# Two attention layers on one core: order of the two products that fill a tile of scores

## The chip, the cores and the metric

The kernel runs on one core of a Trainium2 chip. The metric is the device time of one execution in microseconds (us), lower is better. Three executions of the kernel before took 4043.36, 4045.41 and 4047.82 us; the median, 4045.41 us, is what the change is measured against.

## The reference, cut to what matters

Two residual layers are applied to an array of 4 images of 32 by 32 positions with 768 channels in float32. Each layer normalises in groups, makes q, k and v for 12 heads of 64 channels (the second layer also convolves and normalises each of them), and attends over the 1024 positions of an image, with a bias that depends on the row and the column of query and key:

```python
attn = jnp.einsum('bqd,bkd->bqk', q, k) / np.sqrt(HD)
rel_bias_h = jnp.einsum('bhwc,hkc->bhwk', rq, Rh)
rel_bias_w = jnp.einsum('bhwc,wkc->bhwk', rq, Rw)
attn = (attn.reshape(b * NH, h, w, h, w) + rel_bias_h[:, :, :, :, None] + rel_bias_w[:, :, :, None, :]).reshape(b * NH, hw, hw)
attn = jax.nn.softmax(attn, axis=-1)
out = jnp.einsum('bqk,bkd->bqd', attn, v)
```

The score before the softmax is thus a sum of two terms, q by k and a bias. The change concerns the order in which the kernel adds these two.

## The kernel before, in words

The work is cut into 48 pairs of heads (4 images, 2 layers, 6 pairs of 2 heads; 128 partitions hold the 64 channels of both heads). For each pair, `attend` (L614) runs over two halves of 512 queries (index `c`), and in each half over 8 tiles of 128 keys (index `kt`), in two groups of four tiles. So there are 96 halves, 192 groups and 768 tiles.

One tile of scores, `s`, lies in PSUM (pool `ps_s`, two buffers, L75 and L667): 128 keys by 2 heads by 512 queries. TensorE fills it with two products for each head. The first (L669) is q by k: plain float32, 64 channels deep, one head in the upper and one in the lower half of the array's rows. It starts the accumulation. The second (L671) adds the biases: the stationary operand `ones` holds zeros and ones that pick, for a key, its row and its column of the bias table, and the moving operand `bias` holds the tables. Both are of type float32r, and the bias was split (L528) into a high part and a rest, so that one product is exact enough. It closes the accumulation, and its end lets ScalarE take the exponential of the whole tile (`e`, L676). As `s` has two buffers, the third tile of a group waits until the exponential of the first has read its buffer, and the fourth until that of the second has.

The biases come late in a pair's preparation. `positions` (L502) makes them on TensorE from q, ScalarE copies them to `whole` (L522), `split` makes `high` (ScalarE, L533) and the rest (VectorE, L534), and 8 DMAs on GpSimd's queue for each half of the queries (L544) spread them over the partitions of `bias` (two buffers, L538). The first tile of a half needs four of these DMAs, the third two more, the fifth the last two.

The order of the work is written out by hand (`manual_schedule`, L94): TensorE executes the instructions in program order. Each step of `attend` yields, and after each yield pieces of other work (the next pair's projections, `positions`, `split`, the previous image's output projection) are put in from a table of events. So a group of four tiles stands between such pieces. `attend` then goes on to add up `e` on VectorE (L684) and to multiply it by v on TensorE (L690). These products and the projections use the array in two halves of columns and all 128 rows, the tiles of scores two halves of rows and all 128 columns.

Of the kernel before, what the change touches and what calls it, by code (L numbers as in the profile page):

```python
# [45 lines left out]
def two_layers(ctx: ExitStack, tc: tile.TileContext, keep, x_in, wqkv, wproj, rels, windows, vrow, small, const, onehot, picks, out):  # L46
# [19 lines left out]
    nc = tc.nc  # L66
# [12 lines left out]
    def bank(name):  # L79
        return ps_m.tile([P, 512], F32, tag="bank", name=name)  # L80
# [20 lines left out]
    def col(c, lo=0, hi=P):  # L101
        return sm[lo:hi, c : c + 1]
# [511 lines left out]
    def attend(pair, os):  # L614


        q, k, bias = pair.q, pair.k, pair.bias
        os.append(q)
        nonlocal found
        heads = [slice(j * D, (j + 1) * D) for j in range(2)]  # L620

        def more():
            nonlocal found
            if rest:
                found = rest.pop(0)(*found)

        for c in range(T // QC):
            cols = slice(c * QC, (c + 1) * QC)

            def copy(av):  # L630
                weighed = one.tile([P, QC], F32, tag="weighed", name="weighed")
                nc.scalar.copy(weighed, av)  # L632
                return weighed

            def sums(weighed, acc, c=c):

                z = bank("z")
                for j in range(2):
                    nc.tensor.matmul(  # L639
                        z[j * D : (j + 1) * D, :], cst[:, ONES : ONES + D], acc[:, j, :],  # L640
                        start=True, stop=True,
                    )
                at = 2 * (pair.i * (T // QC) + c)
                t = work.tile([P, QC], F32, tag="t", name="t", bufs=1)
                inv = work.tile([P, QC], F32, tag="inv", name="inv", bufs=1)
                nc.scalar.activation(t, z, AF.Copy, accum_out=seen[:, at : at + 1])

                nc.scalar.activation(inv, t, AF.Ln, bias=tiny)
                nc.scalar.activation(inv, inv, AF.Exp, scale=-1.0, accum_out=seen[:, at + 1 : at + 2])
                return weighed, t, inv  # L650

            def result(weighed, t, inv, cols=cols):

                nc.vector.scalar_tensor_tensor(t, t, -1.0, inv, ALU.mult, ALU.mult)
                nc.vector.scalar_tensor_tensor(inv, t, 2.0, inv, ALU.add, ALU.mult)

                if pair.layer:
                    nc.vector.tensor_tensor(inv, weighed, inv, ALU.mult)
                    nc.vector.scalar_tensor_tensor(q[:, cols], inv, col(LN + 4), q[:, cols], ALU.mult, ALU.add)
                else:  # L660
                    nc.vector.tensor_tensor(q[:, cols], weighed, inv, ALU.mult)

            for g in range(0, NKT, 4):
                es = []
                for kt in range(g, g + 4):
                    keys = slice(kt * P, (kt + 1) * P)
                    ps = ps_s.tile([P, 2, QC], F32, tag="s", name="s")  # L667
                    for j, rows in enumerate(heads):
                        nc.tensor.matmul(ps[:, j, :], k[rows, keys], q[rows, cols], start=True, stop=False)  # L669
                    for j, rows in enumerate(heads):  # L670
                        nc.tensor.matmul(  # L671
                            ps[:, j, :], ones[rows, keys], bias[c][rows, kt // 2, :],
                            start=False, stop=True,
                        )
                    e = work.tile([P, 2, QC], F32, tag="e", name="e", bufs=4)
                    nc.scalar.activation(e, ps, AF.Exp)  # L676
                    es.append(e)
                more()
                if g == 0:
                    av = ps_av.tile([P, QC], F32, tag="av", name="av")  # L680
                    acc = work.tile([P, 2, QC], F32, tag="acc", name="acc", bufs=1)
                    nc.vector.tensor_tensor(acc, es[0], es[1], ALU.add)  # L682
                for e in es[2 * (g == 0) :]:
                    nc.vector.tensor_tensor(acc, acc, e, ALU.add)  # L684
                yield
                yield
                for t, e in enumerate(es):
                    kt = g + t
                    for j in range(2):
                        nc.tensor.matmul(  # L690
                            av[j * D : (j + 1) * D, :], pair.vt[:, kt, j * D : (j + 1) * D], e[:, j, :],
                            start=(kt == 0), stop=(kt == NKT - 1),
                        )
                more()
                if g + 4 == NKT:
                    rest.extend((sums, result))
                    found = (copy(av), acc)
                yield
                yield
# [70 lines left out]
    for i, pair in enumerate(pairs):  # L770
        for _ in attend(pair, oss[i // NC]):
            for piece in events.pop(step, ()):
                piece()
            step += 1
# [309 lines left out]
```

## Time and profile before

| what | value |
|---|---|
| median of three runs | 4045.41 us |
| the profiled execution's own time | 4040.44 us |
| span of the profiled execution | 4038.7 us |
| granted TensorE clock, mean | 0.996 |
| TensorE busy with matmuls | 3945.2 us (98%) |
| VectorE, ScalarE, GpSimd busy | 2494.3, 1812.1, 409.8 us (62%, 45%, 10%) |
| q by k, L669 | 3072 records, 831.8 us |
| biases, L671 | 1536 records, 615.6 us |
| exponentials, L676 | 768 of 1023 ns, 781.3 us |

The span lies inside the time of the same execution; 1.7 us lie around it. PE is TensorE's matmul stream, PEld its loads of the stationary operand, which run beside it. A plain float32 product leaves two matmul records, each with a load of its own, a float32r product leaves one: hence 3072 records of q by k and 1536 of the biases for 768 tiles and two heads. A record's length holds waiting inside the array too; distances between starts are the safer reading.

### The profile page before, as it was taken

What the parts mean: (1) busy time and instruction counts of PE and PEld (TensorE: products, weight loads), DVE (VectorE), ACT (ScalarE), POOL (GpSimd) and SP (SyncE); (2) the same over time, 40 slices, a digit from 0 to 9 for tenths busy, and PEclk for the clock granted to TensorE, in tenths of its full rate; (3) what the DMA queues carried; (4) which work ended last, traced back from release to release, by engine and by line L of the source; (5) the groups of instructions that cost most, each with busy time, mean ns of one, the idle gap of its engine ahead of it and who ended that gap; (6) DMA issues with size and microseconds to landing.
All of it is one profiled execution on the core that took longest, in us unless ns stands there. A gap on an engine that the chain in (4) does not pass through costs nothing.

```text
span 4038.7 us, 79929 instructions
## 1 busy us (share of the span) xinstructions
PE 3945.2 (98%) x35098; PEld 1720.3 (43%) x35098; DVE 2494.3 (62%) x2800; ACT 1812.1 (45%) x2669; POOL 409.8 (10%) x776
## 2 busy tenths in 40 slices
PE   7999999999999999999899999999999999999999
PEld 3534444434344444444444344354343444434443
DVE  2455423558489985799633454245575898848883
ACT  2444424545255553455423544244443555525552
POOL 0111100110000110010011110001100011000010
PEclk9999999999999999999999999999999999999999
DMA  5333242221411222212133222422114112131112
GB/s 160 85 112 113 71 128 73 57 65 38 132 48 38 76 52 75 63 49 69 41 103 88 58 70 63 144 58 70 47 53 127 37 43 53 40 104 43 38 47 75
DMA packets 179046, 293.34 MB, mean 73 GB/s; under 512 B 22528, under 2 KB 77952, under 8 KB 178688
## 3 DMA queue, kind: packets, MB, share of 16 engines
q1 hardware_dynamic: 117248, 187.41, 14.8%
q0 software_dynamic: 61440, 100.71, 10.9%
q8 instruction: 279, 4.57, 0.5%
q14 instruction: 79, 0.65, 0.1%
HBM read 153.36 MB, written 34.01 MB: 46 GB/s over the span
## 4 chain that ended last, share of the span: by engine, by line
PE 85%; DVE 8%; ACT 3%; issue 1%; DMA 1%; POOL 0%; DVEq 0%; SPq 0%; ACTq 0%
PE qkv L85 18%; PE av L690 14%; PE s L669 14%; PE proj L85 12%; PE m3m L85 4%; PE m4m L85 4%; PE m1m L85 4%; PE s L671 3%; PE ln_c L85 3%; PE rel L517 3%; PE z L639 2%; DVE shared L459 2%; DVE acc L684 2%; PE m L85 2%; ACT e L676 2%
## 5 line engine op out<-in xcount | busy, mean ns | idle before, releaser
L676 ACT ACTIVATE e<-s 128x1024 f32<-128x1024 f32 x768 | 781.3, 1023 | 529.8 <-PE s L671 503.7
L669 PE MATMUL s<-q,k 64*128 64x512 f32 x3072 | 831.8, 618 | 27.9 <-ACT e L676 22.2
L684 DVE TENSOR_TENSOR acc<-acc,e 128x1024 f32<-128x1024 f32 x576 | 705.4, 1225 | 184.4 <-ACT e L676 133.4
L85 PE MATMUL qkv<-xn,wqkv_t 128*64 128x512 f32 x3648 | 815.6, 596 | 2.8 <-DVE xn L268 2.6
L459 DVE SCALAR_TENSOR_TENSOR shared<-shared,sm 128x1056 f32<-128x1056 f32 x576 | 758.3, 1316 | 14.9
L671 PE MATMUL s<-bias,ones 64*128 64x512 f32 x1536 | 615.6, 794 | 13.9 <-DMA bias<-whole 9.5
L690 PE MATMUL av<-e,vt 128*64 128x512 f32 x2624 | 594.5, 595 | 0.0
L544 POOL DMA_DIRECT2D bias<-high x384 | 204.1, 552 | 3356.5 <-ACT high L533 3097.9
L85 PE MATMUL proj<-q,wproj_t 128*64 128x512 f32 x2304 | 504.9, 593 | 0.0
L85 PEld LDWEIGHTS qkv<-xn,wqkv_t 128*64 128x64 f32 x3648 | 252.9, 137 | 488.5 <-issue 482.6
L669 PEld LDWEIGHTS s<-q,k 64*128 64x128 f32 x3072 | 255.4, 186 | 362.0 <-ACT e L676 210.6
L442 ACT ACTIVATE shared<-qkv,sm 128x512 f32<-128x512 f32 (+1 forms) x288 | 129.2, 501 | 595.6 <-PE qkv L85 595.6
L723 DVE SCALAR_TENSOR_TENSOR x<-proj,pbias,x 128x512 f32<-128x512 f32 x96 | 72.1, 751 | 439.4 <-PE proj L85 435.0
L690 PEld LDWEIGHTS av<-e,vt 128*64 128x64 f32 x2624 | 184.7, 137 | 347.5 <-issue 328.9
L682 DVE TENSOR_TENSOR acc<-e 128x1024 f32<-128x1024 f32 x96 | 117.6, 1225 | 345.4 <-ACT e L676 344.6
L85 PEld LDWEIGHTS proj<-q,wproj_t 128*64 128x64 f32 x2304 | 163.7, 137 | 313.5 <-issue 311.7
L671 PEld LDWEIGHTS s<-bias,ones 64*128 64x128 f32 x1536 | 150.2, 188 | 199.6 <-issue 193.6
L544 POOL DMA_DIRECT2D bias<-whole x384 | 204.9, 562 | 119.5 <-DVE whole L534 109.0
L632 ACT COPY weighed<-av 128x512 f32<-128x512 f32 x96 | 56.3, 586 | 329.2 <-PE av L690 329.2
L85 PEld LDWEIGHTS ln_c<-cst,shared 128*64 128x64 f32 x2304 | 131.4, 138 | 44.4 <-issue 34.6
L517 PEld LDWEIGHTS rel<-q,rel 64*32 64x32 f32 x6144 | 111.6, 105 | 78.0 <-issue 61.0
L85 PE MATMUL ln_c<-cst,shared 128*64 128x128 f32 x2304 | 139.2, 274 | 3.1 <-DVE shared L459 3.1
(119 smaller groups left out, 3613.0 us busy)
## 6 DMA issues: line engine op xcount, KB each, us to landing
bias<-high POOLq DMA_DIRECT2D x384, 128.0 KB, 2.8
bias<-whole POOLq DMA_DIRECT2D x384, 128.0 KB, 3.0
wqkv_t<-in_wqkv SPq DMA_DIRECT2D x78, 384.0 KB, 3.1
wqkv_t<-mixed SPq DMA_DIRECT2D x66, 384.0 KB, 3.1
wproj_t<-in_wproj SPq DMA_DIRECT2D x48, 384.0 KB, 3.7
wqkv_t<-in_wqkv SPq DMA_DIRECT2D x66, 192.0 KB, 2.5
xn<-in_x SPq DMA_DIRECT2D x24, 512.0 KB, 7.8
x<-in_x SPq DMA_DIRECT2D x48, 256.0 KB, 2.8
```

Of the source, the lines that this page charges most:

```text
L85: nc.tensor.matmul(ps[lo : lo + D], a[:, lo : lo + D], b, start=start, stop=stop, **kw)
L442: nc.scalar.activation(self.pad[s][:, rows, there : there + src.shape[2]], src, AF.Identity, bias=col(self.column(s)))
L459: nc.vector.scalar_tensor_tensor(y, window, tap, y, ALU.mult, ALU.add)
L517: nc.tensor.matmul(ps[lo : lo + S, k * S : (k + 1) * S].rearrange("p (b c) -> p b c", b=2), rel[rows, 2 * self.layer + i, first : first + ...
L544: nc.gpsimd.dma_start(sets, some.unsqueeze(1).to_broadcast([D // 2, 2, QC]))
L639: nc.tensor.matmul(z[j * D : (j + 1) * D, :], cst[:, ONES : ONES + D], acc[:, j, :], start=True, stop=True,)
L669: nc.tensor.matmul(ps[:, j, :], k[rows, keys], q[rows, cols], start=True, stop=False)
L671: nc.tensor.matmul(ps[:, j, :], ones[rows, keys], bias[c][rows, kt // 2, :], start=False, stop=True,)
L676: nc.scalar.activation(e, ps, AF.Exp)
L682: nc.vector.tensor_tensor(acc, es[0], es[1], ALU.add)
L684: nc.vector.tensor_tensor(acc, acc, e, ALU.add)
L690: nc.tensor.matmul(av[j * D : (j + 1) * D, :], pair.vt[:, kt, j * D : (j + 1) * D], e[:, j, :], start=(kt == 0), stop=(kt == NKT - 1),)
```

## The change

The biases' product of both heads is put ahead of q by k in each tile. It now opens the accumulation, and q by k closes it. Nothing is added or removed; the four matmuls of a tile, their operands and all that stands around the tile stay as they were.

```diff
@@ -666,12 +666,12 @@
                     keys = slice(kt * P, (kt + 1) * P)
                     ps = ps_s.tile([P, 2, QC], F32, tag="s", name="s")
                     for j, rows in enumerate(heads):
-                        nc.tensor.matmul(ps[:, j, :], k[rows, keys], q[rows, cols], start=True, stop=False)
-                    for j, rows in enumerate(heads):
                         nc.tensor.matmul(
                             ps[:, j, :], ones[rows, keys], bias[c][rows, kt // 2, :],
-                            start=False, stop=True,
+                            start=True, stop=False,
                         )
+                    for j, rows in enumerate(heads):
+                        nc.tensor.matmul(ps[:, j, :], k[rows, keys], q[rows, cols], start=False, stop=True)
                     e = work.tile([P, 2, QC], F32, tag="e", name="e", bufs=4)
                     nc.scalar.activation(e, ps, AF.Exp)
```

After the change the biases' product stands on L669 to L672 and q by k on L674. Compiled, the order of instructions on VectorE, ScalarE, GpSimd and SyncE is the same as before; on TensorE the matmuls of each tile change places. The waits move with the places: the wait for a free buffer of `s` and the waits for the biases' DMAs now stand together on the first biases' product of a tile.

## Prediction

> **What bounds the kernel now.** I read the page first (busy time, chain, groups), then the timeline of an ordinary group of tiles, then the waits on the biases' line, then the timeline of a tile whose biases came late.
>
> ```profile
> PE 3945.2 (98%) x35098; PEld 1720.3 (43%) x35098; DVE 2494.3 (62%) x2800; ACT 1812.1 (45%) x2669; POOL 409.8 (10%) x776
> ...
> PE 85%; DVE 8%; ACT 3%; issue 1%; DMA 1%; POOL 0%; DVEq 0%; SPq 0%; ACTq 0%
> ...
> L676 ACT ACTIVATE e<-s 128x1024 f32<-128x1024 f32 x768 | 781.3, 1023 | 529.8 <-PE s L671 503.7
> L669 PE MATMUL s<-q,k 64*128 64x512 f32 x3072 | 831.8, 618 | 27.9 <-ACT e L676 22.2
> ```
>
> TensorE is busy for 98% of the span and carries 85% of the chain that ended last; ScalarE has room. So what lengthens TensorE's stream lengthens the kernel, and what only makes ScalarE start later costs where TensorE waits for it. An ordinary group (start, length):
>
> ```profile
> 2606.86 0.60 PE L85 MATMUL proj<-q,wproj_t 128*64 128x512 f32 x2
> 2607.38 0.30 PEld L669 LDWEIGHTS s<-q,k 64*128 64x128 f32 x4 [0.81 <-issue]
> ...
> 2607.92 0.19 PEld L671 LDWEIGHTS s<-bias,ones 64*128 64x128 f32 x2 [0.24 <-issue]
> ...
> 2608.35 0.42 PEld L669 LDWEIGHTS s<-q,k 64*128 64x128 f32 x4 [0.23 <-issue]
> 2608.58 1.02 PE L669 MATMUL s<-q,k 64*128 64x512 f32 x4
> 2608.78 2.12 ACT L676 ACTIVATE e<-s 128x1024 f32<-128x1024 f32 x2 [5.85 <-PE s L671]
> ...
> 2609.86 0.30 PEld L669 LDWEIGHTS s<-q,k 64*128 64x128 f32 x4 [0.66 <-ACT e L676]
> ...
> 2612.24 0.19 PEld L639 LDWEIGHTS z<-acc,cst 128*64 128x64 f32 x3 [0.56 <-issue]
> ```
>
> Here are four intervals. From the group's first load to the first exponential: 2608.78 - 2607.38 = 1.40 us. The exponential (1.02) and 0.05 of release later, at 2609.86, the third tile begins: it waits for ScalarE, so a later first exponential makes a later third tile. From there to the first load of other work: 2612.24 - 2609.86 = 2.38. And at the top, the end of float32 work: from the last start (2606.86) to a load in another arrangement of the array 0.52; the reader of that product (VectorE, in the same window) starts at 2607.50, 0.64 after. Over all 192 groups the two tile intervals have medians of 1.40 and 2.38; in 72 groups the first is longer, since ScalarE is still on other work. Which late biases there are, from the answer for L671:
>
> ```profile
>   DMA bias<-high: 10.2, 5
>   DMA bias<-whole: 9.5, 4
> ```
>
> 19.7 us over nine waits, always the first tile of a pair. One of them:
>
> ```profile
> 407.91 1.13 PE L669 MATMUL s<-q,k 64*128 64x512 f32 x4
> ...
> 411.08 0.21 PEld L671 LDWEIGHTS s<-bias,ones 64*128 64x128 f32 x2 [2.87 <-issue]
> 411.11 0.50 PE L671 MATMUL s<-bias,ones 64*128 64x512 f32 x2 [2.07 <-DMA bias<-whole]
> 411.19 0.45 PEld L669 LDWEIGHTS s<-q,k 64*128 64x128 f32 x4
> 411.41 1.02 PE L669 MATMUL s<-q,k 64*128 64x512 f32 x3
> ...
> 411.64 2.11 ACT L676 ACTIVATE e<-s 128x1024 f32<-128x1024 f32 x2 [3.03 <-PE s L671]
> ...
> 411.88 0.59 PE L669 MATMUL s<-q,k 64*128 64x512 f32 x1
> ```
>
> q by k ran at 407.91, inside the wait for the DMA; after the landing only the biases' pass was left: 411.64 - 411.08 = 0.56 to the exponential. This is also the one place where the trace shows a biases' product with nothing ahead of it, as each group will begin after the change: from its load to the last q by k start of the product behind it 411.88 - 411.08 = 0.80.
>
> **What the Trainium skill says.** "FP8 and Floating Point Precision", TensorE Precision Notes: true float32 takes four passes, the reduced form reads a truncated value. The trace agrees: two float32 records lie 0.43 apart (two passes each), the biases' pass takes 0.23 at most (2608.35 to 2608.58). "TensorE: Matmul & The Clock Gate", Step-by-step: loads are pulled ahead of running matmuls, matmuls keep program order. The trace agrees: q's load at 2608.35 runs under the biases' pass; and keeping order means that a biases' product which waits holds up q by k behind it. "TensorEngine Tiling (Array Packing)", Key Properties: a change of the tiling mode drains the array. The trace agrees: 0.52 from a last float32 start to the next mode's load, where its passes take 0.43. "TensorE: Matmul & The Clock Gate", What's actually happening: after an idle window of about 3.4 us the clock halves until a busy one. The trace's clock record has stretches of 3.41 us at 0.5, among them just after the waits at 57 and 3930 us.
>
> **The change part by part.**
>
> *Passes.* A tile keeps two float32 records and one pass per head; in an unbroken run tiles follow every 1.09 us (exponentials at 1.09), in either order. Cost nothing; what differs is the two ends and the waits.
>
> *Group start to first exponential.* Before 1.40. After: a biases' load with nothing ahead, 0.80 to the last q by k start, then 0.64 to the reader: 1.44. The 0.80 holds 0.03 by which the second head trailed the first there (it trails by 0.01 elsewhere). Whether it trails so where there was no DMA wait, no row shows: 1.41 to 1.44. Raising every group's interval to these values, those where ScalarE is late anyway left as they are, gives 1.3 to 4.9 us over 192 groups.
>
> *Third tile to the next work.* Before 2.38. After: 0.80 + 1.09 (the fourth tile) + 0.52 = 2.41, without the trailing 2.38. Times 192: 0 to 6.3 us. The weight load of the fourth tile's biases is released by the second exponential, as q's was; it is late by at most 0.01, up to 1.5 us. With the line above: 1.3 to 12.7 us. I take 8, the trailing in the tiles that stand behind a wait and not in all others.
>
> *Late biases.* I laid the landing of the DMAs beside the first load of every tile that needs them. In ten pairs the last of the four landed after the tile's start. In six (3.0 to 5.4 us late, one 1.0) q by k filled the wait; now it comes after: load to exponential 0.57 becomes 1.44, 0.87 each, 5.2 us. In four, 0.5 us late, the biases' load stood 0.59 after the start and was wholly hidden under q by k (exponential still at 1.40). Now 0.59 + 1.44 - 1.40 = 0.63 each, 2.5 us. Sum 7.8 us (7.7 before rounding each). Queued behind the waiting instruction on TensorE are q by k, the other tiles, and all later pieces; ScalarE's exponential and VectorE's sums wait for it. The next-closest landing is 4.0 us ahead of its tile: no other pair is touched. All third and fifth tiles have at least 2 us.
>
> *The clock.* With q by k gone from the wait TensorE idles about 1 us longer in the six. Two of these already end at half clock (a 3.41 us window at half speed costs at most 1.7 us); three others idle 2.0, 2.0 and 2.9 us now and 3.0 to 3.9 then. Bounds 0 to 5.1 us; I take one new window, 1.7.
>
> *What may be gained.* Four first tiles wait 2.2 us in all for k (ScalarE, L419); a biases' pass may run under such a wait, at most 4 x 0.23 = 0.9 us, but two of the four are late-bias pairs where it can't. I count nothing. The biases' buffer comes free a product earlier for GpSimd's DMAs; they feed the second half of the queries, which has slack. Other DMAs and queues are not moved past anything.
>
> *Waits of the sequencer.* The extra event waits for the DMAs (four per half, 0.05 us each in the trace) stood behind q by k and were hidden. They now stand at the tile's head; TensorE's sequencer was seen about 0.5 us ahead of the array, so I count nothing. If the cover is gone: 384 x 0.05 = 19.6 us.
>
> *Sum.* 8 + 7.8 + 1.7 = 17.5 us. On the profiled execution, 4040.4 (span 4038.7 and 1.7 around it), that is 4057.9; that execution lies 5.0 under the median of the runs shown, so against the median 4045.4 + 17.5 = 4062.9, said as 4063.
>
> **The rivals.** A measurement of this kernel can tell about 0.2%, 8.1 us, from no change.
>
> *Not slower: the order is neutral and the lost cover is given back.* Place: the ten late tiles. If TensorE after such a tile soon has to wait for ScalarE or VectorE anyway (93 us of the span are idle), the 7.8 us vanish into that wait; with no trailing the group part is 1.3, and up to 0.9 is gained at k. It decides once less than half of the late-tile cost survives and no trailing shows. For it: 72 groups are held by ScalarE. Against: in nine of the ten the third tile began 1.08 after the first exponential began, released by it, so the delay is passed on. Time 4045.4 + 1.3 = 4047; chance 0.20, most within 0.2%, 0.03 faster.
>
> *More: event waits exposed.* At a group's head behind tiny matmuls (40 groups follow `positions`) the sequencer may have no lead. With half of the 19.6 us and all three clock windows: 8 + 7.8 + 5.1 + 9.8 = 30.7, 4076. Chance 0.12. Against: the trace shows the lead.
>
> *The change is not done.* The compiled order on TensorE shows the products swapped in all tiles; I give it nothing.
>
> **How the numbers follow.** Forecast 4063 with 0.68 (its bounds 9.1 to 25.6 us: 4054 to 4071), not slower 4047 with 0.20, more 4076 with 0.12. Slower by over 0.2%: 0.68 + 0.12 = 0.80; within: 0.17; faster: 0.03. Range 4048 to 4075: it leaves out about 0.12 of the rival below and 0.07 above.
>
> **What would show it.** In the profile after: the exponential's releaser is q by k; group start to exponential 1.41 to 1.44, third tile to next work 2.38 to 2.41 (trailing or not); a late tile's biases' load to exponential 1.44 where it was 0.57; waits on the biases' DMAs in ten first tiles totalling about 27 us where nine made 19.7 (six grow by 0.96, the load and two passes that ran inside them, and the four of 0.5 show); one to three more half-clock stretches. I am wrong if the group intervals shrink, if landings move with the order, or if event waits show at tile heads.

## The result, and the profile after

The changed kernel takes 4052.34 us (median of 15 runs, 4048.41 to 4055.28), the kernel before, timed beside it, 4043.36 us (15 runs, 4040.16 to 4047.82). The ratio is 1.0022, with a 95% interval of 1.0014 to 1.0029: 9.0 us slower, between 5.7 and 11.7. The forecast was 17.5 us slower. The profiled execution took 4052.07 us with a span of 4050.2 us, 11.5 us over the span of before.

The page after, the lines that answer to those of before:

```profile
PE 3946.5 (97%) x35098; PEld 1717.0 (42%) x35098; DVE 2494.8 (62%) x2800; ACT 1811.2 (45%) x2669; POOL 410.0 (10%) x776
...
PE 84%; DVE 9%; ACT 3%; DMA 2%; issue 2%; POOL 0%; DVEq 0%; SPq 0%; ACTq 0%
```

TensorE's busy time grew by 1.3 us, the span by 11.5: the difference is mostly idling, and DMA has gone from 1 to 2% of the chain that ended last. An ordinary group, the one that was shown of before (start, length), in which ScalarE's exponentials are now released by q by k (L674):

```profile
2616.42 0.60 PE L85 MATMUL proj<-q,wproj_t 128*64 128x512 f32 x2
2616.95 0.19 PEld L669 LDWEIGHTS s<-bias,ones 64*128 64x128 f32 x2 [0.81 <-issue]
...
2617.29 1.02 PE L674 MATMUL s<-q,k 64*128 64x512 f32 x4
...
2618.36 2.11 ACT L676 ACTIVATE e<-s 128x1024 f32<-128x1024 f32 x2 [5.86 <-PE s L674]
...
2619.43 0.19 PEld L669 LDWEIGHTS s<-bias,ones 64*128 64x128 f32 x2 [0.87 <-ACT e L676]
...
2621.80 0.20 PEld L639 LDWEIGHTS z<-acc,cst 128*64 128x64 f32 x4 [0.76 <-issue]
```

First load to first exponential: 2618.36 - 2616.95 = 1.41 us (before 1.40). Third tile to the next work: 2621.80 - 2619.43 = 2.37 (before 2.38). From the group's first load to the next work it is 4.85 us here and 4.86 before; over all groups but those behind a late wait the median is 4.86 in both kernels. The order of the two products is free here. The waits on the biases' line:

```profile
  DMA bias<-whole: 18.2, 9
  DMA bias<-high: 11.4, 3
```

This is 29.6 us in the view where it was 19.7. Neither sum is the time lost: pair 0 stands twice in each, with its weight load and with its matmul, and three of the nine waits of before (one of the twelve after) are waits of about 0.2 us in other tiles. Counted once, on the matmuls of the first tiles, five tiles waited 13.9 us before and ten wait 23.7 us after.

A pair is called late where the last of the four DMAs that its first tile needs lands after that tile's start in the trace of before. There are ten; in six of them (pairs 0, 5, 23, 24, 29 and 47) the wait is deep, 1.0 us or more, and in four it is 0.5 us. The late tile that was shown of before (pair 5):

```profile
409.28 0.21 PEld L669 LDWEIGHTS s<-bias,ones 64*128 64x128 f32 x2 [3.95 <-issue]
409.31 0.50 PE L669 MATMUL s<-bias,ones 64*128 64x512 f32 x2 [3.10 <-DMA bias<-whole]
...
409.62 1.87 PE L674 MATMUL s<-q,k 64*128 64x512 f32 x4
...
411.52 1.02 ACT L676 ACTIVATE e<-s 128x1024 f32<-128x1024 f32 x1 [4.67 <-PE s L674]
```

From the biases' load to the exponential 411.52 - 409.28 = 2.24 us, where before it was 0.56. The four q by k that follow the load take 1.87 us, where the same four take 1.02 in the ordinary group. The cause is the clock. The view of stretches of the same execution shows it (length; busy time of PE, PEld, DVE, ACT and POOL; granted clock; DMA share; GB/s):

```profile
409.70:413.10 3.40, 3.40 (x14) 1.71 (x10) 3.30 (x3) 1.02 (x1) 2.11 (x5) 0.50 0.96 245
```

The granted clock is 0.50 right after the wait. The clock record of a trace holds such stretches at 0.50, each of 3.41 us or a small multiple of it, but for the one at the trace's end; they are called half-clock stretches below, and their sums are taken over the profiled execution.

I followed the start of each group's last exponential from one trace to the other. The kernel after falls behind at all ten late pairs: these ten steps add up to 14.2 us. Between them the distance mostly stands still; from pair 9 to pair 22 it changes by less than 0.1 us over 54 groups. Against the 14.2 stand some -3 us net at seven other groups, two of which lose 1.2 and 1.3 us and the others gain. Half-clock stretches lie there in one execution and not in the other (the one at 325 us in the trace of before has no counterpart after), and waits for VectorE change. At 325.65 us of before, a product of the preparations had waited 2.93 us for VectorE (L330); after, at 326.31, it waited 2.02. So 0.9 of the 1.6 us that had been lost until then vanished in a wait that was there anyway.

### The profile page after: what moved, and what is told of

Its sections match the earlier page's. It is cut to its first block, busy times and chain, and to the rows that moved or that the text cites. A ratio compares the mean times of both kernels' runs of the same rounds, so it can differ in the third digit from the quotient of the medians.

```text
span 4050.2 us, 79929 instructions
## 1 busy us (share of the span) xinstructions
PE 3946.5 (97%) x35098; PEld 1717.0 (42%) x35098; DVE 2494.8 (62%) x2800; ACT 1811.2 (45%) x2669; POOL 410.0 (10%) x776
## 4 chain that ended last, share of the span: by engine, by line
PE 84%; DVE 9%; ACT 3%; DMA 2%; issue 2%; POOL 0%; DVEq 0%; SPq 0%; ACTq 0%
PE qkv L85 18%; PE av L690 13%; PE s L674 12%; PE proj L85 12%; PE s L669 5%; PE m4m L85 4%; PE m3m L85 4%; PE m1m L85 4%; PE ln_c L85 3%; PE rel L517 2%; DVE shared L459 2%; DVE acc L684 2%; PE z L639 2%; PE m L85 2%; ACT e L676 2%
## 5 line engine op out<-in xcount | busy, mean ns | idle before, releaser
L674 PE MATMUL s<-q,k 64*128 64x512 f32 x3072 | 793.8, 594 | 1.1 <-issue 1.1
L669 PE MATMUL s<-bias,ones 64*128 64x512 f32 x1536 | 456.4, 589 | 51.7 <-ACT e L676 21.0
L669 PEld LDWEIGHTS s<-bias,ones 64*128 64x128 f32 x1536 | 147.0, 186 | 454.1 <-ACT e L676 285.6
L674 PEld LDWEIGHTS s<-q,k 64*128 64x128 f32 x3072 | 297.3, 188 | 84.4 <-issue 49.8
```

The costliest lines, as they stand in the source:

```text
L669: nc.tensor.matmul(ps[:, j, :], ones[rows, keys], bias[c][rows, kt // 2, :], start=True, stop=False,)
```

## The experiments

Theory 1, formed on the two traces: the whole cost sits in the ten first tiles whose biases come late; the q by k that filled the wait now follows it, and the longer idling brings stretches of half clock. The rivals: a cost in every group, as the prediction's largest term had it, masked by something else; or the clock alone. Each run was timed beside the kernel before, on the same chip, and its ratio is the one to that kernel.

**1 and 2. The old order in the first tile of a pair alone, and the new order there alone.** Both kernels have the two products as functions and choose for each tile:

```diff
+                    a, b = (biases, scores) if c or kt else (scores, biases)
+                    a(True, False)
+                    b(False, True)
```

> The changed kernel, with the old order (q by k first) in the first tile of each of the 48 pairs alone; 720 of 768 tiles keep the biases first. Theory 1 (the whole cost sits in the ten first tiles whose biases come late, about 0.87 us in six and 0.63 in four, plus the clock after longer idling): 4043.4, as the kernel before, within 2 us either way; the half-clock stretches are those of before (33 us in all). Rival (a cost or gain in every group of tiles, that something else offsets): 3 us or more away from the kernel before.

Measured: 4041.43 us against 4042.52, ratio 0.9998 (0.9990 to 1.0007), half-clock stretches 33.0 us in all (32.7 before). 720 of the 768 tiles have the new order and no cost can be seen: the interval is -4.0 to 2.8 us, which excludes the 8 us of the prediction's largest term, though not 1 or 2 us. The second has `not (c or kt)` in its condition:

> The kernel before, with the new order in the first tile of each of the 48 pairs alone. Theory 1: the full cost of the change, 4052 (+9, of it 7.7 from the waits). Rival (cost in every group): at most a part, the ten waits without the group's share, 4048 or less.

Measured: 4055.26 us, ratio 1.0028 (1.0018 to 1.0039), that is 11.3 us by the ratio (7.3 to 15.8) and 12.7 by the medians: the whole cost of the change, within the intervals. Half-clock stretches: 48.5 us (48.4 in the changed kernel). Its waits on the biases' line add up to 30.2 us in the same view (18.6 and 11.6), 29.6 in the changed kernel.

So the cost is in the 48 first tiles, and the rival with a cost of several us spread over all groups falls.

**3 and 4. More late pairs.** Both kernels with the split of the second layer two steps later:

```diff
-                (12, lambda: self.split()),
+                (14, lambda: self.split()),
```

> The kernel before, with the split of the biases two steps later in the 24 pairs of the second layer, so that the DMAs land some 3 us after their first tile's start in all of them. Slower than before by the waits, 40 to 80 us. It is the partner of the next run; only their difference tells something.

> The changed kernel, with the same later split. Theory 1 (0.87 us for each late pair): slower than its partner by 22 x 0.87 more than the change alone, that is by some 27 us, plus a few us for half-clock stretches. Rival (cost in every group, or a clock effect alone): slower by about 9, as without the late split.

Measured: 4074.93 us with q by k first (ratio 1.0077, 1.0063 to 1.0090) and 4101.55 with the biases first (1.0144, 1.0128 to 1.0159). The first is slower by 32 us, less than the 40 to 80 I wrote. The difference of the partners, 26.6 us, is the 27 expected, but the number of pairs behind it was not: the DMAs came late in 18 more pairs, not 22, 28 in all (24 deep, 4 of 0.5 us). At 0.86 and 0.62 us each (below) that is 23.1 us; the half-clock stretches went from 49.6 to 74.4 us and can make the rest. Laid beside each other as above, the two traces part by 28.5 us at the 28 late pairs and by 1.2 us at all other groups together. The matmuls of the first tiles wait 67.5 us for DMAs with the biases first and 37.5 with q by k first (118.9 and 70.1 in the view, which counts some tiles twice). Cost follows the number of late pairs: 9.0 us with ten, 26.6 with 28.

**5. Work in the wait, one product.** In the changed kernel, ahead of the first tile's biases in the six pairs with a deep wait, stands a q by k whose result is overwritten:

```diff
+                    if not (c or kt) and pair.i in (0, 5, 23, 24, 29, 47):
+                        for j, rows in enumerate(heads):
+                            nc.tensor.matmul(ps[:, j, :], k[rows, keys], q[rows, cols], start=True, stop=True)
```

> The changed kernel; in the first tile of the six pairs with a deep wait a q by k whose result is overwritten runs ahead of the biases, so that TensorE works inside the wait as it did before the change, while the useful q by k still comes after. Theory 1: the 7.7 us of the waits stay, the half-clock stretches go back from 48 us to about 33; 4050 to 4051. Rival (the clock alone makes the cost): back to 4043.

Measured: 4051.88 us, ratio 1.0019 (1.0012 to 1.0026): the cost of the change stays. But the half-clock stretches only fell to 40.2 us, not to the 33 expected, and five of the six tiles still ended at half clock. So the run neither supports the rival "the clock alone" nor excludes it, and it doesn't separate clock and wait; 9 and 10 do in part.

**6 and 7. The DMAs that the first tile needs first.** In `split`, in the changed kernel and in the one before:

```diff
-                for part, src in enumerate((high, self.whole)):
-                    for i in range(2):
-                        for h in range(2):
+                for h in range(2):
+                    for part, src in enumerate((high, self.whole)):
+                        for i in range(2):
```

> The changed kernel, with the eight DMAs of a half of the queries issued in another order: the four that the first tile needs stand first, so the last of them is issued up to three places (0.51 us each) sooner, and at least one. Theory 1: the four waits of 0.5 us vanish (2.5 us), the six deep ones shrink by 0.5 to 1.5 us each (3 to 9 us): 4041 to 4047. Rival (what costs is the order in every group): 4052.

> The kernel before, with the same order of DMAs. Theory 1: the four waits of 0.5 us were hidden, so only the six deep ones gain: 3 to 9 us faster than before, 4034 to 4040; faster than its partner by some 5 to 6 us. Rival: no difference to the kernel before.

Measured: 4043.39 us with the biases first (ratio 1.0001, 0.9993 to 1.0010) and 4037.87 with q by k first (0.9986, 0.9980 to 0.9993), the kernel before, timed beside them, 4044.3. Landing sooner takes 9 us off the changed kernel, as much as the change had cost. The order has not become free by that: the partners lie 5.5 us apart, as expected. With q by k first the four waits of 0.5 us had nothing to gain, as they were hidden already. The second kernel beats both the kernel before and the changed one.

**8. Two q by k in the wait.** The kernel of 7, and in the six pairs q by k of the first two tiles ahead of the first tile's biases:

```diff
+                    if not c and kt < 2 and pair.i in (0, 5, 23, 24, 29, 47):
+                        if kt == 0:
+                            pss = [ps_s.tile([P, 2, QC], F32, tag="s", name="s") for _ in range(2)]
...
+                        ps = pss[kt]
```

> The kernel before with the same order of DMAs, and in the six pairs with a deep wait q by k of the first and second tile ahead of the first tile's biases. Theory 1 (what fills the wait is free): up to 0.86 us less for each of the six against the run before this one where the wait is still longer than both, 3 to 5 us: 4030 to 4037. Rival: the third tile waits for a first exponential that doesn't come sooner, so nothing is gained.

Measured: 4040.30 us, ratio 0.9992 (0.9984 to 1.0000): no gain on 7. Pair 5 in this kernel:

```profile
406.84 0.33 PEld L681 LDWEIGHTS s<-bias,ones 64*128 64x128 f32 x4 [1.56 <-issue]
...
407.41 1.94 ACT L686 ACTIVATE e<-s 128x1024 f32<-128x1024 f32 x2 [2.58 <-DVE acc L694]
...
408.49 0.30 PEld L679 LDWEIGHTS s<-q,k 64*128 64x128 f32 x4 [1.32 <-ACT e L686]
```

The first exponential comes 0.57 us after the biases' load, as in the kernel before, and the third tile waits for it (1.32 us of idling). Theory 1's expectation fell here, and the rival's reason holds here: what fills a wait is worth something only as far as it makes the first exponential earlier. In pair 24 the wait was no longer there, and the second product only delayed its first exponential.

**9 and 10. The whole wait filled.** As many q by k with an overwritten result as fit into each deep wait, in the changed kernel and in the one before:

```diff
+                    for _ in range({0: 5, 5: 3, 23: 4, 24: 1, 29: 3, 47: 3}.get(pair.i, 0) if not (c or kt) else 0):
+                        for j, rows in enumerate(heads):
+                            nc.tensor.matmul(ps[:, j, :], k[rows, keys], q[rows, cols], start=True, stop=True)
```

> The changed kernel; in the six pairs with a deep wait, one to five q by k whose result is overwritten run ahead of the first tile's biases, as many as fit into the wait, so that TensorE hardly idles there. Theory 1 with a clock share: landing to second exponential 1.53 + 1.09 in all ten late pairs, 7.7 us more than the partner below, 4048 to 4051, below the changed kernel by the clock's 1 to 4 us. Rival (no clock share in the times): 4052.

> The kernel before, with its waits filled in the same way by two to four q by k whose result is overwritten. Theory 1: landing to first exponential 0.67 in six and 0.92 in four late pairs, 7.7 us faster than its partner; against the kernel before 0 to 4 us faster by the half-clock stretches that go.

Measured: 4042.13 us with the biases first (ratio 0.9998, 0.9989 to 1.0006) and 4038.53 with q by k first (0.9991, 0.9983 to 1.0000; here 4, 2, 3, 2 and 2 products in pairs 0, 5, 23, 29 and 47). Pair 5 with the biases first, and the granted clock after the wait:

```profile
408.69 0.21 PEld L672 LDWEIGHTS s<-bias,ones 64*128 64x128 f32 x2 [1.20 <-issue]
408.72 0.50 PE L672 MATMUL s<-bias,ones 64*128 64x512 f32 x2 [0.40 <-DMA bias<-whole]
...
410.11 2.11 ACT L679 ACTIVATE e<-s 128x1024 f32<-128x1024 f32 x2 [3.93 <-PE s L677]
```

```profile
408.70:412.10 3.40, 3.35 (x18) 1.68 (x18) 3.19 (x4) 1.92 (x2) 2.43 (x5) 1.00 1.01 250
```

Load to exponential is 1.42 us instead of 2.24, at a clock of 1.00. Laid beside the landing of the last DMA, the first exponential comes 1.53 us after it in all ten late pairs, and the second 1.09 later. With q by k first and full clock it is 0.67 in the deep ones (pair 23 apart) and 0.91 to 0.97 in the four of 0.5 us. That is the pure cost of the order: 0.86 and 0.6 us. In the two profiled executions the steps at the ten late pairs add up to 6.1 us, and the spans lie 5.4 us apart. The partners lie 3.6 us apart in the medians, less than the 7.7 expected. Part of that is my filling: in pair 23 the third product overran the landing and cost the partner 1.1 us. The intervals of the two ratios are each about 3.5 us wide to either side, so the rest is not settled. With the wait filled the changed kernel takes 10 us less and is level with the kernel before, so the clock has a large share. Its size can't be read from this: the filling also takes away stretches that the kernel before has (22.0 us are left with the biases first, 32.7 in the kernel before), and the partner, filled too, is still faster.

**11. Both together.** The kernel of 7, with its remaining deep waits filled (1, 4, 1 and 2 products in pairs 5, 23, 29 and 47).

> The kernel before with the four DMAs that the first tile needs issued first, and with its four remaining deep waits filled by one to four q by k whose result is overwritten. If the shorter waits and the full clock add up: 4032 to 4036, faster than either alone (4037.9 and 4038.5). If both live from the same half-clock stretches: 4036 to 4039.

Measured: 4034.30 us, ratio 0.9980 (0.9971 to 0.9989). The two add up within their intervals (0.14 and 0.09% alone, 0.20% together). It is the fastest of the study, 8.8 us under the kernel before that was timed beside it (4043.07) and some 18 under the changed one.

## Why the prediction was right or wrong, point by point

- **Direction and place: right.** Slower was forecast with 0.80. Which pairs would lose was read off before the change ran: ten late pairs, no other, and the third and fifth tiles untouched. Runs 1 and 2 show, within their intervals, that the first tiles hold the whole cost.
- **Passes: right.** Exponentials still follow each other every 1.09 us, in either order.
- **Group start and third tile: the step that failed.** The step gave 1.3 to 12.7 us and took 8, for "the trailing in the tiles that stand behind a wait and not in all others". The trace after has 1.41 and 2.37 us, the lower ends of both intervals. The loads of the two heads' biases start 0.003 us apart in ordinary groups and behind waits for ScalarE. They start 0.03 apart in the late tiles, the one place in which the trace of before showed a biases' product with nothing ahead of it, and in 19 groups that follow `positions`, where the first exponential comes no later than before. The prediction carried what it saw behind a late DMA over to other waits. The term measured nothing: 1.41 at the start is given back at the end (2.37 for 2.38), and run 1 has 0.9998. Almost half of the forecast was this term.
- **Late biases: right, 7.6 of 7.8 us.** With the clock full (run 9), landing to first exponential goes from 0.67 to 1.53 in six (0.86 each; 0.87 was forecast) and from 0.91 to 1.53 in four (0.62; 0.63 was forecast). The sum of the waits was misread, without an effect on the forecast: the 19.7 us of before are not nine first tiles but five (pair 0 twice) and three other tiles. So the 27 us expected and the 29.6 of the view are not ten waits; those are 23.7 us, some 10 more than before. Likewise the "four first tiles" that wait 2.2 us for k are two, pairs 23 and 47, each counted with load and matmul.
- **The clock: right in kind, too small in size.** One new window, 1.7 us, was taken, and 5.1 was the upper bound. In the profile five of the six deep tiles run at half clock, four from their first product on and pair 5 from its q by k on. Landing to second exponential, added over the six, is 24.7 us after and 12.1 before. Less 6 x 0.86 that leaves 7.5 us for the clock, beyond the bound. The bound failed because it counted only windows new after the change: two stretches that began behind the tile before now begin in front of it, and most last 6.83 us instead of 3.41.
- **The sum.** 0 for the groups, 7.6 for the waits and 7.5 for the clock make 15.1 in the two profiled executions; 3.6 us go off elsewhere (half-clock stretches of the kernel before that are gone, shorter waits for VectorE), which gives the 11.5 of the spans. The medians say 9.0. So two errors partly cancelled: 8 us too many for the groups, several too few for the clock. Without its group term the forecast would have been 9.5 us. That this lies near 9.0 is in part luck, since the clock cost more than was taken and other places gave some back.
- **Waits of the sequencer, k, the buffer: nothing was counted, and they cost nothing.** No event wait shows at a tile's head in the group above, nor in the flat distance between late pairs. In the 19 groups behind `positions` with which a half begins, the first biases' product starts, counted from the matmul ahead of it, 0.03 us later than the first q by k did before (0.06 to 0.15 in four of them), but the first exponential is at most 0.01 later in any.
- **The rivals.** The not-slower one failed at its own point: the delay of the late tiles was passed on to the third tile each time. Its mechanism is real but small here, the 0.9 us taken up by the wait for VectorE at 325 us. The event waits of the other rival cost nothing; its three new clock windows did show.

How much of the 9.0 us is clock in the median execution stays open. Half-clock stretches lie elsewhere in each execution, and 9 and 10 together leave the split between waits and clock uncertain by some 5 us.

## What to carry to other kernels

When two products fill one tile and one operand arrives late, put the one whose operands are there first: in the steady state the order costs nothing, and at a late arrival the whole other product moves behind it. Find the place by laying the landings beside the first use, not by the busy share; here ten tiles of 768 decided. Count the clock after a longer wait as well as the delay itself: in the profiled executions here it was half of the loss (7.5 of 15.1 us). Work with a discarded result in the wait took as much off the changed kernel (4042.1 us) as issuing first the transfers that the first tile needs (4043.4 us); the second removes the cause, and the two together were fastest.

## What the runs showed of the hardware that had not been expected

- Behind a wait for a DMA, the weight loads of the two heads' float32r products start 0.03 us apart, and the q by k of the two heads behind them 0.03 to 0.04 apart; behind a wait for ScalarE both are 0.003 apart. The two float32r products themselves start 0.003 apart in either case.
- The half-clock stretches lie on a grid of 3.413 us in each trace (at 62.2 and at 236.3 us before, 51 steps apart), at another offset in each execution. Whether an idle stretch costs anything depends on how it lies in that grid. In pair 5 the matmuls idle 2.07 us ahead of the biases in the kernel before and 2.10 in run 5. Before, a step ends inside that wait, so the idling of the pair is split over two steps, and the clock stays full. In run 5 it lies in one step, and the next step is at half clock. The steps of before and then of run 5 (length; busy time of PE, PEld, DVE, ACT and POOL; granted clock; DMA share; GB/s):

```profile
406.96:410.37 3.41, 2.08 (x10) 0.44 (x6) 3.31 (x4) 0.59 (x1) 3.04 (x6) 1.00 0.55 113
410.37:413.78 3.41, 2.64 (x14) 1.27 (x14) 3.20 (x4) 2.05 (x2) 3.19 (x7) 1.00 0.95 230
```

```profile
408.78:412.19 3.41, 1.31 (x9) 0.91 (x10) 3.20 (x3) 0.00 (x0) 3.41 (x7) 1.00 0.91 206
412.19:415.60 3.41, 3.41 (x16) 1.78 (x12) 2.95 (x3) 2.05 (x2) 1.13 (x3) 0.50 0.86 220
```

- Counted so in all 13 traces from 25 us on, by the matmul records: every step at full clock with 2.0 us of idling or more was followed by one at half clock, and none with less than 1.76 (102 changes to half clock; of the steps in between, 12 were followed by half clock and 24 were not). A step at half clock was followed by full clock where it idled 0.61 us or less, and by half clock again where it idled 0.63 or more (126 steps). So a step need not be idle throughout to halve the clock, as the prediction took it.
- One product (0.86 us) at the front of a wait did not keep the clock; filling the wait (0.40 us of idling left in pair 5) did.
